# Selective scan in a four-layer kernel: softplus split between ScalarE, TensorE and VectorE, its steps placed anew, and one fill shared differently

## The chip, the cores and the metric

The kernel runs on one core of a Trainium2 chip. The metric is the device time of one launch in microseconds; lower is better. The engines are named as the profile names them: PE is TensorE, DVE is VectorE, ACT is ScalarE, POOL is GpSimd, SP is SyncE, which here only issues transfers (DMAs).

## The reference

The reference takes an image batch of 3 x 256 x 48 x 48 in fp32 through four layers, each added to its own input: an attention block with feed-forward parts, a 3 x 3 convolution with routed weights, a plain 3 x 3 convolution, and a state space (selective scan) layer. The change lies in the last one. Cut to what matters:

```python
xz = einsum('blc,dc->bld', layer_norm(group_norm(x)), in_proj_w)     # L = 2304 tokens, 256 channels
x_in, z = split(xz)                                                  # 512 inner channels each
u  = silu(causal_conv4(x_in))
dt_raw, B_ssm, C_ssm = split(u @ x_proj_w.T)                         # 16 + 16 + 16
dt = softplus(dt_raw @ dt_proj_w.T + dt_proj_b)                      # 512 channels
for t:                                                               # 16 states per channel
    h = h * exp(dt[t] * A) + dt[t] * B_ssm[t] * u[t]
    y[t] = (h * C_ssm[t]).sum(states)
out = ((y + u * D) * silu(z)) @ out_proj_w.T
```

The softplus of a value a is computed as max(a, 0) + ln(1 + exp(-|a|)).

## The kernel before, in words

Three layers come first and take the span up to about 2,020 us. The scan layer then works through 18 chunks (three images, six chunks of CH = 384 tokens each). The 512 inner channels are four blocks of 128 (m = 0 to 3). A block is taken in two steps (h = 0 and 1), so a chunk has eight steps; each step holds eight scans ("parts", g over two groups, q over four quarters of the block's channels), so that a partition of a scan holds one state of one channel.

In a step, ACT computes `decay` (exp of dt times A, L1811) into one of three PSUM slots, three parts ahead; DVE runs the recurrence as one scan instruction per part (L1819) in the tile `hs`; POOL multiplies the eight results by C (`times_c`, L1836); PE folds the products into `ps_y` (`add_states`, L1853). The input term dt*u*B of the next step is put into `hs` by `fill` at the end of a step: DVE fills the quarters 0 and 1 (`fill_upper`, L1765) from PSUM, POOL the quarters 2 and 3 (L1785). In the second step of a block POOL also does a part of DVE's share, the "second fill" (L1780), from a copy of the rows (`spread_second`, DMA `dtuq`). The rows of dt and dt*u reach the layout of the scan over DRAM: `keep_dt` stores them (`dtd`, `dtud`), `spread` loads them replicated (`dtr`, `dtur`), `spread_pe` does a part by PE.

Beside the scans of chunk `at`, the next chunk (rel = 1) and the one after it (rel = 2) are prepared. The list `plan` says where: an entry (j, place, rel, stage) puts a stage at half step j (0 to 15; j = 4m + 2h + part // 4), at a place BEGIN, MID, DONE, LATE (after the parts 0, 1, 2, 3 of that half step), or PE_ (after part 3 of a step, or, for odd j, at the end of the step). The stages that matter here are `group_scale` (L1213), `less_mean` (L1222), `centre` (L1235, L1237), `square_mean` (L1229), `inverse_root` (L1241, L1242) and `normalise` (L1246) for rel = 2, and `project_dt` (L1318), `softplus` (L1327 to L1329), `take_dt` (L1343, L1344) and `keep_dt` (L1349 and two DMAs) for rel = 1, the last four twice, for the blocks 0, 1 (m0 = 0) and 2, 3 (m0 = 2). All of them use the same two PSUM banks, `bank[0]` and `bank[1]` (in the profile `ps_g`): a stage that writes a bank follows the readers of the one before.

`keep_busy` (L1336) are filler matmuls with no result that is used; the table `busy` says after which parts they come. At the end `keep_order` ties the instructions of PE, DVE, ACT and POOL in this stage to the order in which the program lists them. SP's order is left to the planner of the framework. [...] Before the stage, the first chunk is prepared by another function with the same `softplus` and `take_dt`.

## Time and profile before

| | |
|---|---|
| median of 3 runs | 3367.3 us (3366.03 to 3369.35) |
| the profiled execution, its own time | 3369.11 us |
| its span | 3367.4 us |
| granted PE clock, mean | 0.978 |
| busy share of the span: PE, DVE, ACT, POOL | 94%, 86%, 71%, 40% |
| scan stage, 2018 to 3345 us: busy PE, DVE, ACT, POOL | 1199.7, 1311.0, 1098.4, 1283.5 us |
| one chunk in the stage (start to start of L1246) | 73.87 us |

The shares of the whole span mix the stages; POOL's 40%, for one, comes almost wholly from the last 1,330 us. Times of single instructions are durations, and consecutive instructions of an engine overlap somewhat, so that the distance from start to start is the cost of one. "Idle before" and an arrow name what an engine was waiting for.

### The profile page before, as it was taken

Reading aid. Unit: us, or ns where it says so; the run is one execution under the profiler, and the core shown is the slowest. Engines: PE = TensorE matmul, PEld = TensorE weight load, DVE = VectorE, ACT = ScalarE, POOL = GpSimd, SP = SyncE. Lnnn points to the kernel's source line nnn. Section 1 sums busy time; section 2 is a strip of 40 time slices with the busy share of each in tenths; the row PEclk is TensorE's granted clock in tenths of the full one; section 3 lists DMA queues with packets and bytes.
Section 4 is the critical chain, followed back from the end, with each engine's and each line's share of the span. In section 5 each row is a group of like instructions: output and inputs, shape, how many; then the busy total and the mean of one; then the engine's idle time right before and its main releaser. Section 6 shows DMA issues by size and latency. Waiting matters only on the chain.

```text
span 3367.4 us, 54979 instructions
## 1 busy us (share of the span) xinstructions
PE 3159.9 (94%) x21314; PEld 1591.0 (47%) x21314; DVE 2892.8 (86%) x3302; ACT 2376.1 (71%) x3596; POOL 1346.1 (40%) x457
## 2 busy tenths in 40 slices
PE   7999999999999999979999997999999999999995
PEld 4334343352333434547777763444444444444442
DVE  3799989958989998369975459999999999999997
ACT  2688888838888886331324447888888888888874
POOL 0000000000000000220000009999999999999997
PEclk9999999999999999989999999999999999999987
DMA  4000000010000002566611135455555555555552
GB/s 165 31 8 10 8 8 6 8 46 5 8 7 8 10 8 71 174 217 216 216 31 38 38 105 122 120 125 131 134 130 140 135 127 128 133 127 137 133 133 56
DMA packets 182164, 290.84 MB, mean 86 GB/s; under 512 B 34737, under 2 KB 148465, under 8 KB 179970
## 3 DMA queue, kind: packets, MB, share of 16 engines
q1 hardware_dynamic: 168658, 267.15, 29.4%
q10 hardware_dynamic: 13232, 20.06, 1.8%
q8 instruction: 169, 2.77, 0.4%
q14 instruction: 105, 0.86, 0.1%
HBM read 236.24 MB, written 50.64 MB: 85 GB/s over the span
## 4 chain that ended last, share of the span: by engine, by line
PE 52%; DVE 32%; ACT 7%; DMA 5%; issue 4%; SPq 1%; POOL 0%; ACTq 0%; DVEq 0%; POOLq 0%
DVE hs L1819 21%; PE ps_s L638 16%; PE acc L651 14%; PE ps_c L1546 8%; DVE hs L1765 3%; PE ps_s L1031 2%; DVE u L296 2%; PE ps_y L462 2%; ACT ps_da L1811 2%; PE ps_m L665 1%; PE ps_m L711 1%; PE acc L529 1%; PE ps_s L518 1%; DVE ps_g L1343 1%; PE ps_s L578 1%
## 5 line engine op out<-in xcount | busy, mean ns | idle before, releaser
L642 ACT ACTIVATE pt<-ps_s 128x1024 f32<-128x1024 f32 x972 | 942.5, 1022 | 154.6 <-PE ps_s L638 142.1
L1819 DVE TENSOR_TENSOR_SCAN hs<-ps_da,hs 128x385 f32<-128x385 f32 x1152 | 1002.1, 935 | 4.2 <-ACT ps_da L1811 1.5
L857 DVE TENSOR_TENSOR part<-part,pt 128x2048 f32<-128x2048 f32 x396 | 906.6, 2289 | 41.2 <-ACT pt L642 18.4
L1811 ACT ACTIVATE ps_da<-dtr,u 128x384 f32<-128x384 f32 x1152 | 656.6, 582 | 184.3 <-DVE hs L1819 175.7
L164 POOL TENSOR_TENSOR rstd<-ve,mhalf 128x2 f32<-128x2 f32 (+1 forms) x26 | 16.3, 629 | 1480.3 <-DVE ve L162 1480.3
L638 PE MATMUL ps_s<-q,kt 32*128 32x512 f32 (+1 forms) x4320 | 576.4, 592 | 0.1
L651 PE MATMUL acc<-pt,vt 128*32 128x512 f32 (+1 forms) x4320 | 520.9, 561 | 0.2
L1546 PE MATMUL ps_c<-vt,u 128*128 128x288 f32 x1728 | 432.4, 411 | 20.6 <-DVE u L263 20.6
L1836 POOL TENSOR_TENSOR hc<-hs,x 128x3072 f32<-128x3072 f32 x72 | 405.3, 5629 | 19.2 <-DVE hs L1819 15.2
L1836 POOL TENSOR_TENSOR hc<-hs,bc 128x3072 f32<-128x3072 f32 x71 | 399.9, 5633 | 15.9 <-DVE hs L1819 14.2
L1546 PEld LDWEIGHTS ps_c<-vt,u 128*128 128x128 f32 x1728 | 330.8, 192 | 117.1 <-issue 19.4
L638 PEld LDWEIGHTS ps_s<-q,kt 32*128 32x128 f32 x4320 | 195.2, 183 | 199.1 <-issue 120.2
L651 PEld LDWEIGHTS acc<-pt,vt 128*32 128x32 f32 x4320 | 94.4, 108 | 353.4 <-issue 326.7
L1853 PE MATMUL ps_y<-hc,u 128*32 128x384 f32 x2304 | 230.4, 521 | 2.8 <-POOL hc L1836 2.8
L1273 PE MATMUL ps_g<-u 128*128 128x384 f32 x576 | 195.2, 491 | 23.5 <-ACT u L1269 23.5
L1785 POOL TENSOR_TENSOR hs<-dtur,x 128x1536 f32<-128x1536 f32 x72 | 209.2, 2905 | 9.1 <-DMA dtur<-dtud 8.5
L1785 POOL TENSOR_TENSOR hs<-dtur,bc 128x1536 f32<-128x1536 f32 x72 | 209.3, 2907 | 1.1 <-DMA dtuq<-dtud 1.1
L1273 PEld LDWEIGHTS ps_g<-u 128*128 128x128 f32 x576 | 108.3, 191 | 107.2 <-ACT u L1269 34.7
L1336 PE MATMUL ps_r<-hs,ident 128*128 128x128 f32 x864 | 130.7, 292 | 19.8 <-DVE hs L1819 19.5
L1336 PEld LDWEIGHTS ps_r<-hs,ident 128*128 128x128 f32 x864 | 107.6, 192 | 73.8 <-DVE hs L1819 56.1
L1853 PEld LDWEIGHTS ps_y<-hc,u 128*32 128x32 f32 x2304 | 62.4, 113 | 145.0 <-issue 129.6
L1562 ACT COPY cb<-ps_c 128x288 f32<-128x288 f32 x48 | 19.2, 399 | 157.5 <-PE ps_c L1546 137.9
(266 smaller groups left out, 4062.8 us busy)
## 6 DMA issues: line engine op xcount, KB each, us to landing
wconv<-in_we SPq DMA_DIRECT2D x144, 384.0 KB, 4.4
dtr<-dtd SPq DMA_DIRECT2D x288, 192.0 KB, 3.9
dtur<-dtud SPq DMA_DIRECT2D x288, 96.0 KB, 4.2
wconv<-xd SPq DMA_DIRECT2D x36, 384.0 KB, 3.7
x<-bcd SPq DMA_DIRECT2D x72, 192.0 KB, 5.0
dtd<-x SPq DMA_DIRECT2D x36, 384.0 KB, 2.9
dtuq<-dtud SPq DMA_DIRECT2D x288, 48.0 KB, 2.0
bc<-bcd SPq DMA_DIRECT2D x72, 192.0 KB, 4.9
```

The lines of the kernel that those rows point to most:

```text
L638: nc.tensor.matmul(s[:, j, cols], kt[r, mt * P : (mt + 1) * P], q[r, :n], start=True, stop=True,)
L642: nc.scalar.activation(p[:, h0 : h0 + 2, :], s, AF.Exp)
L651: nc.tensor.matmul(acc[h * HD : (h + 1) * HD, :n], vt[:, mt, g * P + h * HD : g * P + (h + 1) * HD], p[:, h, cols], start=mt == 0, stop=mt ...
L857: ): nc.vector.tensor_tensor(part, first, p, ALU.add)
L1273: nc.tensor.matmul(bank[m % 2], w3v["taps"][:, m, tap, :], w3v["xi"][:, m % 3, tap : tap + CH], start=tap == 0, stop=tap == DCONV - 1,)
L1336: nc.tensor.matmul(spread_tiles[-1][:, i % 2, CH:], ident, src, start=True, stop=True)
L1546: nc.tensor.matmul(pc[:, :HN], u[:, i, dy, ct, m * P : (m + 1) * P], vt[:, i, ct, dy * TW : dy * TW + HN], start=ct == 0 and dy == 0, stop ...
L1785: nc.gpsimd.tensor_tensor(states(s)[:, :, 2:4, 1:], chunks[at].rows[m][1].unsqueeze(1).broadcast_to([P, 2, 2, CH]), b_rows(s, 0, 2), ALU.mult,
L1811: nc.scalar.activation(slots[n % 3][:, 1 : CH + 1], chunks[at].rows[m][0][:, q, :], AF.Exp, scale=amat[:, col : col + 1],)
L1819: nc.vector.tensor_tensor_scan(b, slots[(8 * s + part) % 3][:, : CH + 1], b, 0.0, ALU.mult, ALU.add)
L1836: nc.gpsimd.tensor_tensor(hc, tiles[s][:, :, :, 1:], cb.broadcast_to([P, 2, 4, CH]), ALU.mult)
L1853: nc.tensor.matmul(k.y_ps[32 * q : 32 * q + 32, :CH], fold, hc[:, g, q, :], start=False, stop=h == 1 and g == 1,)
```

## The change

In the scan stage `softplus` and `take_dt` are replaced by smaller stages. ACT writes the positive part max(a, 0) to the tile `dtu` (Relu) and |a| to `dt`; the exponential and the logarithm follow in place. PE adds the two by products with the identity matrix into the same banks (`sum_dt`, first the positive part, then the logarithm). DVE then only multiplies the bank by u (`take_sum`). The positions in the plan change with it: for m0 = 0 the bank is taken and stored at the end of the sixth step instead of in its first half; for m0 = 2 in the seventh step after part 4. `take_sum` stands ahead of `keep_dt`, as `take_dt` did. The first chunk, ahead of the stage, keeps `softplus` and `take_dt`, the latter without its fillers.

`group_scale` goes from the seventh step (one call for both halves) to the fourth, a half in each half step. `less_mean` moves from the end of the seventh step's first half to part 5 of that step. In the eighth step POOL's second fill covers one group instead of two, as in the other steps, and DVE's part of the fill ahead of it two quarters instead of one. Fillers go: those of `take_dt`, and eight of the 24 in the table. Both stores of B and C rows are issued ahead of the loads, and `keep_order` now covers SP as well.

```diff
-    def group_scale(k):
+    def group_scale(k, *cts):
         sc, sh = norm3[k.b]
-        for ct in range(CT):
+        for ct in cts or range(CT):
...
             nc.sync.dma_start(bcd[j], dbc[32 * (j + 1) : 32 * (j + 1) + DS, :])
+        for j in range(2):
             t = room(k, f"bc{j}")
...
+    def relu_of(k, m0):
+        for j in range(2):
+            nc.scalar.activation(k.dtu[:, m0 + j, :], bank[j], AF.Relu)
+
+    def abs_of(k, m0):
+        for j in range(2):
+            nc.scalar.activation(k.dt[:, m0 + j, :], bank[j], AF.Abs)
+
+    def relu_abs(k, m0):
+        for j in range(2):
+            nc.scalar.activation(k.dtu[:, m0 + j, :], bank[j], AF.Relu)
+            nc.scalar.activation(k.dt[:, m0 + j, :], bank[j], AF.Abs)
+
+    def exp_of(k, m0):
+        both = k.dt[:, m0 : m0 + 2, :]
+        nc.scalar.activation(both, both, AF.Exp, scale=-1.0)
+
+    def log_of(k, m0):
+        both = k.dt[:, m0 : m0 + 2, :]
+        nc.scalar.activation(both, both, AF.Ln, bias=1.0)
+
+    def sum_dt(k, m0, part):
+        src = (k.dtu, k.dt)[part]
+        for j in range(2):
+            nc.tensor.matmul(
+                bank[j], ident, src[:, m0 + j, :], start=part == 0, stop=part == 1
+            )
+
+    def take_sum(k, m0):
+        for j in range(2):
+            m = m0 + j
+            nc.vector.tensor_tensor(k.dtu[:, m, :], bank[j], k.u[:, m, :], ALU.mult)
...
             nc.vector.scalar_tensor_tensor(pdt, pdt, 0.0, k.dt[:, m, :], ALU.max, ALU.add)
             nc.vector.tensor_tensor(k.dtu[:, m, :], pdt, k.u[:, m, :], ALU.mult)
-            keep_busy(k.dtu[:, m, :P], 3)
...
-        (12, MID, 2, group_scale),
-        (12, PE_, 2, less_mean),
+        (6, BEGIN, 2, lambda k: group_scale(k, 0)),
+        (7, BEGIN, 2, lambda k: group_scale(k, 1)),
+        (13, MID, 2, less_mean),
         (13, DONE, 2, centre),
...
-        (9, LATE, 1, lambda k: softplus(k, 0)),
-        (10, DONE, 1, lambda k: take_dt(k, 0)),
-        (10, LATE, 1, lambda k: keep_dt(k, 0)),
-        (10, PE_, 1, lambda k: project_dt(k, 2)),
-        (11, LATE, 1, lambda k: softplus(k, 2)),
-        (12, MID, 1, lambda k: take_dt(k, 2)),
-        (12, DONE, 1, lambda k: keep_dt(k, 2)),
+        (9, DONE, 1, lambda k: relu_of(k, 0)),
+        (9, LATE, 1, lambda k: abs_of(k, 0)),
+        (10, BEGIN, 1, lambda k: sum_dt(k, 0, 0)),
+        (10, DONE, 1, lambda k: exp_of(k, 0)),
+        (11, BEGIN, 1, lambda k: log_of(k, 0)),
+        (11, MID, 1, lambda k: sum_dt(k, 0, 1)),
+        (11, LATE, 1, lambda k: take_sum(k, 0)),
+        (11, LATE, 1, lambda k: keep_dt(k, 0)),
+        (11, PE_, 1, lambda k: project_dt(k, 2)),
+        (11, PE_, 1, lambda k: relu_abs(k, 2)),
+        (11, PE_, 1, lambda k: exp_of(k, 2)),
+        (12, BEGIN, 1, lambda k: sum_dt(k, 2, 0)),
+        (12, BEGIN, 1, lambda k: log_of(k, 2)),
+        (12, MID, 1, lambda k: sum_dt(k, 2, 1)),
+        (13, BEGIN, 1, lambda k: take_sum(k, 2)),
+        (13, BEGIN, 1, lambda k: keep_dt(k, 2)),
...
-        busy = {(2, 0, 3): 4, (2, 1, 1): 3, (2, 1, 2): 3, (2, 1, 3): 3, (2, 1, 5): 3,
-                (3, 0, 0): 3, (3, 0, 1): 3, (3, 0, 2): 2}
+        busy = {(2, 0, 3): 4, (2, 1, 1): 2, (2, 1, 2): 2, (2, 1, 3): 3, (2, 1, 4): 3,
+                (3, 0, 3): 2}
...
                 fill_upper(s, 0, 2)
-                fill_upper(s + 1, 0, 1, 1 if m == DI - 1 else 2)
+                fill_upper(s + 1, 0, 1)
             else:
                 fill_upper(s, 1, 2, 1)
-                lo = 0 if m == DI - 1 else 1
                 nc.gpsimd.tensor_tensor(
-                    states(s)[:, lo:2, 1, 1:],
-                    chunks[at].second[m].unsqueeze(1).broadcast_to([P, 2 - lo, CH]),
-                    chunks[at].bc[0][:, 2 + lo : 4, :], ALU.mult,
+                    states(s)[:, 1, 1, 1:], chunks[at].second[m],
+                    chunks[at].bc[0][:, 3, :], ALU.mult,
                 )
...
-        keep_order(tc, listed, mark)
+        keep_order(tc, listed, mark, True)
...
-def keep_order(tc, listed, mark):
+def keep_order(tc, listed, mark, loads=False):
...
-    )
+    ) + ((mybir.EngineType.SP,) if loads else ())
```

## The prediction

> **What bounds the kernel now.** I read the page first: its slices show the last fifteen (2,020 us on) with DVE and POOL both at nine tenths. The changed functions run there. So the shares over the whole span decide nothing; that stretch does. Next the busy time by stretches (columns: stretch, length, busy time and count of PE, weight loads, DVE, ACT, POOL, then granted clock, DMA share, GB/s):

> ```profile
> 2600.00:2800.00 200.00, 186.81 (x922) 96.52 (x922) 198.46 (x239) 169.77 (x335) 193.52 (x54) 1.00 0.55 133
> 2800.00:3000.00 200.00, 185.09 (x938) 97.77 (x937) 198.36 (x244) 166.92 (x329) 193.74 (x56) 0.99 0.55 134
> ```

> The reader is to see that DVE is full (99%), and that the next two are close: POOL 97%, PE 93%. ACT has 84%. A microsecond taken from DVE counts until one of these stops it. Successive starts of the normalise line L1246 (2683.5, 2757.4, 2831.3 us) give the clock of the stage: one chunk every 73.87 us.

> Then the timeline of DVE over the third step pair of a chunk and what follows (start, length of the run, engine, line, count):

> ```profile
> 2804.81 2.65 DVE L1819 TENSOR_TENSOR_SCAN hs<-ps_da,hs 128x385 f32<-128x385 f32 x3
> 2807.64 0.57 DVE L1343 SCALAR_TENSOR_TENSOR ps_g<-ps_g,x 128x384 f32<-128x384 f32 x1 [0.18 <-ACT x L1329]
> 2808.24 0.56 DVE L1344 TENSOR_TENSOR dtu<-ps_g,u 128x384 f32<-128x384 f32 x1
> 2808.71 0.56 DVE L1343 SCALAR_TENSOR_TENSOR ps_g<-ps_g,x 128x384 f32<-128x384 f32 x1
> 2809.30 0.56 DVE L1344 TENSOR_TENSOR dtu<-ps_g,u 128x384 f32<-128x384 f32 x1
> 2809.78 4.35 DVE L1819 TENSOR_TENSOR_SCAN hs<-ps_da,hs 128x385 f32<-128x385 f32 x5
> 2814.04 0.53 DVE L1860 TENSOR_TENSOR x<-ps_y,x 128x384 f32<-128x384 f32 x1
> 2814.49 2.21 DVE L1765 TENSOR_TENSOR hs<-ps_r,x 128x1536 f32<-128x1536 f32 x2
> ```

> Instructions overlap, so what one costs is the distance of starts, not its duration: a scan 0.852 us (duration 0.935), the L1343/L1344 quartet 9.78 - 7.64 = 2.14 us, of which two L1344 take 0.47 each and two L1343 0.60. There is no idle time but 0.18 us.

> POOL at the end of the same chunk, and ACT and PE around the hand-over that the change makes later:

> ```profile
> 2819.88 1.55 POOL L1780 TENSOR_TENSOR hs<-dtuq,x 128x768 f32<-128x768 f32 x1
> 2821.39 2.91 POOL L1785 TENSOR_TENSOR hs<-dtur,x 128x1536 f32<-128x1536 f32 x1
> 2825.82 5.63 POOL L1836 TENSOR_TENSOR hc<-hs,x 128x3072 f32<-128x3072 f32 x1 [1.53 <-DVE hs L1819]
> ```
> ```profile
> 2822.48 2.85 PE L1222 MATMUL ps_g<-wconv,u 128*128 128x384 f32 x8 [0.31 <-ACT x L1349]
> ```
> ```profile
> 2825.36 0.85 ACT L1235 COPY wconv<-ps_g 128x384 f32<-128x384 f32 x2
> 2826.24 0.84 ACT L1237 ACTIVATE wconv<-wconv 128x768 f32<-128x768 f32 x1
> 2826.99 0.57 ACT L1811 ACTIVATE ps_da<-dtr,u 128x384 f32<-128x384 f32 x1
> ```

> POOL waits once a chunk, 1.53 us, for DVE: that is its whole slack. Eight matmul rows of a 384-wide product take 2.85 us, and the page counts two rows per product, so one product costs 0.71 us. The four products of less_mean (L1222) so end at 2825.33, and centre's copies (L1235) begin at 2825.36 behind a decay: nothing waits there now, but with no room to spare.

> [...] two Abs of L1327 take 0.85 us, 0.43 each; I price Relu at that. [...] POOL's L1836 stays at 5.63 us; so I price no contention. [...] The 3 us stretch from 2805 shows 0.57 while the rest of this chunk shows 1.00: [...] rival B rests on it.

> **The change part by part**, per chunk in microseconds; the dt work of a next chunk runs 17 times in the stage, the fills 18 times.

> 1. The positive part and the sum leave DVE. Four L1343 go: twice 2.14 becomes twice 0.97 (two products of bank and u, at L1344's 0.47 to 0.49): **-2.34**. The 0.18 wait for Ln goes if the sum is ready (below): **-0.18**.
> 2. Second fill. In the eighth step POOL's L1780 shrinks from 1.55 to the 0.87 of the other steps (-0.68 POOL); DVE's second L1765 before it grows from 384 to 768 per partition. In the same trace the pair takes 2.13 (2814.49 to 2816.62) where it has 384 and 2.53 where it has 768: **+0.40 DVE**, 18 times.
> 3. PE gets eight identity products, 8 x 0.71 = +5.7, and loses fillers: 12 of take_dt and 24 - 16 = 8 of the table, at 1.5 us for six, 20 x 0.25 = -5.0. Net +0.7 on about 69 busy. This lies beside DVE; it would be 69.5 of 72, still under DVE.
> 4. ACT gets four Relu, 4 x 0.43 = +1.7, on 62: 64 of 72. Group scaling (two L1213, 1.29) moves from the seventh step to the fourth; there decays run at most three scans ahead, and after the scan of part 4 ACT has a slack of about one scan (0.85) per 0.65 us inserted, so I cost it nothing; if that cover is gone, the Silu and its two table loads behind it (4.05) come up to 0.6 late, in front of a fill of 2.5.
> 5. Order on SP. It now follows the program. Both bcd stores stand ahead of all eight bc loads, and four dtuq loads behind them instead of two on each side: 0.83 of issue moves about 3.7 later. Those rows are next read by POOL over 10 us later. The dtd and dtud stores of blocks 0 and 1 move from the sixth step's middle to its end, directly ahead of the spread loads of the next chunk. Store 2.9 to 4.5, eight issues 3.7, load 3.9 to 4.3 (page): 12 to 15 us from the end of the sixth step. First reader is the decay for the next chunk, late in the eighth: by the pitches 2.5 + 0.97 + 2.53 + 6.82 + 0.97 + 5 = about 19. Hidden. What it replaces was a queue that stood: before, SP's 17 waits for L1349 lasted 109.8 us in the 600 us from 2600.
> 6. New waits. dt*u of blocks 0, 1 follows the sixth step's last scan. Ln follows the decay of part 4, ends about 1.5 after that scan, and two products give bank 1 at +3.0; DVE gets there after three scans and the gate, at +3.0. No wait, margin about 0.1. For blocks 2, 3 (seventh step, after scan 4) the sum is ready some 0.3 early. Then the bank is copied by ACT (L1349, 0.85) and only then less_mean may write it: four products, 2.85. From scan 4's end: decay 0.7, first copy 1.1, products to 4.0; centre's second copy is due at 3.7. ACT so stands 0.3 to 0.5 and the decay behind centre and square comes that much later. In the trace before, this decay ended 0.15 before its scan: the wait reaches DVE. I take **+0.45**; ends 0 (less_mean keeps ahead) and +1.2 (the standing repeats at inverse_root, whose square_mean is behind it).

> POOL's floor by starts: 8 x 5.59 + 8 x 2.86 + 4 x 0.83 = 70.9. DVE's: 64 x 0.852 + 4 x 2.53 + 4 x 0.45 (fills) + 4 x 0.45 (gates) + 0.85 (L1246) + 1.94 = 71.0 before any wait. They touch: DVE gains nothing below 71, and without the halved second fill POOL would have needed 71.6.

> Sum: 17 x (-2.34 - 0.18 + 0.45) + 18 x 0.40 = -35.2 + 7.2 = **-28.0 us**, a chunk of 72.2. The profiled execution took 3369.11 us (span 3367.4 and 1.7 around it); the median of the runs is 3367.3, 1.8 lower. So 3341.1 for a profiled run, **3339 us** for the median.

> **Rivals.**
> A, above (0.70): DVE stays the bound; with the ends of the new wait, -15 to -36, so 3331 to 3352.
> B (0.13), gain cut short: the fillers that are gone let PE's clock fall in another 3 us stretch of the sixth and seventh steps, where PE is busy only 9.7 of 12 us (2814 to 2826) and waits on ACT. At half speed that delays PE by up to 1.5 us; DVE has about 0.3 of margin at the sums, so some 1.2 more per chunk, 17 x 1.2 = 20: about 3359, at the edge of no change. Against: eight real products fill the same place. With POOL at its floor it ends similarly.
> C (0.13), slower: ACT's queue. From less_mean through centre, square, square_mean and inverse_root ACT waits for PE three times with the decays behind it. If less_mean starts 2 us late, say behind the second sum's products and add_states, centre stands that long, and each chunk gets 2.0 + 0.45 of stall where it won 2.1. It decides from a stall of 2.1 per chunk; at 3.0, 17 x 0.9 = +15: 3382. For it: PE is at 100% for 27 us before (2772 to 2799), so a delay is recovered slowly. Against: PE's idle time is precisely in these two steps.
> D (0.04): the order by program gives the same placement of DVE work but SP stands behind a store and the spread loads land late; the -28 is eaten: 3367.

> **How the numbers follow.** A measurement of this kernel tells about 0.2%, 6.7 us: faster is below 3360.6. A gives 0.70 there, B about 0.10, together 0.80; same is the rest of B and most of D, 0.06; slower C and a little of D, 0.14. The range 3327 to 3363 takes A's ends, 4 us for the pitches on the low side, and B; C is left out, 0.14, and about 0.04 below.

> **What would show it.** L1246's later line should start every 72.2 us (71.7 without new waits). DVE: no scalar_tensor_tensor in the stage, products of about 0.47 between starts, a wait ahead of the scans of the eighth step near 0.5. POOL's 1.53 wait in the seventh step should all but vanish. A stage longer than 73.9 per chunk with ACT idle for ps_g ahead of centre shows C; a clock below 0.9 in the sixth and seventh steps shows B; a DVE product that waits for PE's sum by over 0.5 refutes point 6.

## The result, and the profile after

The changed kernel takes 3336.7 us (median of four runs, 3329.3 to 3338.9) against 3366.7 for the kernel before on the same chip: a ratio, estimated from all runs, of 0.9906, 95% interval 0.9892 to 0.9919. The profiled execution has a span of 3333.4 us, 34.0 less than before.

The 34.0 us lie in three places. The scan stage, from the semaphore just ahead of DVE's first fill to DVE's first product with C in the last step, went from 1328.4 us (2016.6 to 3345.0) to 1300.5 (2012.1 to 3312.6): **-27.9 us**. It began 4.5 us earlier, and 1.6 us are saved behind it. In the fourteen kernels of the table below, whose earlier layers are the same, the stage began anywhere from 2007.8 to 2017.1 us, so those 4.5 us are scatter. The stage length of a profile is therefore the finer measure for what follows; it comes from one execution each.

By stretches, in the columns of the table shown before:

```profile
2600.00:2800.00 200.00, 188.40 (x906) 94.43 (x898) 198.69 (x238) 178.02 (x355) 197.70 (x58) 1.00 0.55 132
2800.00:3000.00 200.00, 189.58 (x884) 94.48 (x884) 197.59 (x235) 174.29 (x342) 196.38 (x57) 0.99 0.53 131
```

DVE is as full as before (99%); POOL went from 97% to 98.5%, ACT from 84% to 88%, PE from 93% to 94.5%. Successive starts of normalise are 72.25 us apart on average where they were 73.9. But the distances are of two kinds: ten of fifteen lie at 71.8 to 72.0, five at 72.8 or 72.9.

A chunk of the short kind, DVE's timeline from the end of the sixth step into the eighth:

```profile
2863.46 1.02 DVE L1355 TENSOR_TENSOR x<-ps_g,x 128x384 f32<-128x384 f32 x2
2864.39 2.62 DVE L1808 TENSOR_TENSOR hs<-ps_r,bc 128x1536 f32<-128x1536 f32 x2
2866.91 4.36 DVE L1860 TENSOR_TENSOR_SCAN hs<-ps_da,hs 128x385 f32<-128x385 f32 x5
2871.18 1.01 DVE L1355 TENSOR_TENSOR x<-ps_g,x 128x384 f32<-128x384 f32 x2
2872.09 2.66 DVE L1860 TENSOR_TENSOR_SCAN hs<-ps_da,hs 128x385 f32<-128x385 f32 x3
2874.66 0.55 DVE L1808 TENSOR_TENSOR hs<-ps_r,bc 128x384 f32<-128x384 f32 x1
2875.10 1.81 DVE L1860 TENSOR_TENSOR_SCAN hs<-ps_da,hs 128x385 f32<-128x385 f32 x2
2877.18 3.69 DVE L1860 TENSOR_TENSOR_SCAN hs<-ps_da,hs 128x385 f32<-128x385 f32 x4 [0.27 <-ACT ps_da L1852]
```

The two products with u (L1355, take_sum) start 0.93 us before what follows them, 0.47 each, with no wait; nothing is left of the scalar_tensor_tensor. The one wait, 0.27 us in the eighth step, is for a decay on ACT. On ACT, at the same moment, the copies of centre wait for PE's less_mean:

```profile
2874.67 0.48 ACT L1235 COPY wconv<-ps_g 128x384 f32<-128x384 f32 x1 [0.15 <-PE ps_g L1222]
2875.32 0.48 ACT L1235 COPY wconv<-ps_g 128x384 f32<-128x384 f32 x1 [0.17 <-PE ps_g L1222]
```

The long kind differs in one instruction: DVE waits for PE's sum in the seventh step.

```profile
2938.88 4.35 DVE L1860 TENSOR_TENSOR_SCAN hs<-ps_da,hs 128x385 f32<-128x385 f32 x5
2944.18 1.20 DVE L1355 TENSOR_TENSOR dtu<-ps_g,u 128x384 f32<-128x384 f32 x2 [0.94 <-PE ps_g L1348]
```

PE's timeline says why. The two chunks have the same instructions, but the fold of the states (L1894, 16 rows) takes 1.50 us in the short chunk and 2.51 in the long one. The eight rows of the sum behind it take 2.85 us in the short chunk and 2.19 + 1.45 in the long one. The first and the third line are the short chunk's:

```profile
2866.90 1.50 PE L1894 MATMUL ps_y<-hc,u 128*32 128x384 f32 x16
2938.87 2.51 PE L1894 MATMUL ps_y<-hc,u 128*32 128x384 f32 x16
2868.33 2.85 PE L1348 MATMUL ps_g<-x,ident 128*128 128x384 f32 x8
2941.30 2.19 PE L1348 MATMUL ps_g<-dtu,ident 128*128 128x384 f32 x4
2943.34 1.45 PE L1348 MATMUL ps_g<-x,ident 128*128 128x384 f32 x4
```

And the granted clock (the third column from the end) in the same two places:

```profile
2868.00:2871.00 3.00, 3.00 (x16) 1.63 (x9) 3.00 (x4) 2.80 (x6) 3.00 (x1) 1.00 0.45 138
2940.00:2943.00 3.00, 3.00 (x15) 1.09 (x8) 3.00 (x4) 2.80 (x6) 3.00 (x2) 0.56 0.75 159
```

In stretches of 1 us the clock falls under 0.8 at 2072, 2144, 2506, 2577, 2939 and 3011 us, and nowhere else between 2060 and 3230. DVE's 0.9 us waits for the sum number six in the stage, one at each of these.

### The profile page after: what moved, and what is told of

The parts are those of the page before. It is cut to its first block, busy times and chain, and to the rows that moved or that the text cites. A ratio compares the mean times of both kernels' runs of the same rounds, so it can differ in the third digit from the quotient of the medians.

```text
span 3333.4 us, 54144 instructions
## 1 busy us (share of the span) xinstructions
PE 3141.3 (94%) x20890; PEld 1555.3 (47%) x20890; DVE 2862.1 (86%) x3234; ACT 2393.7 (72%) x3664; POOL 1334.0 (40%) x457
## 4 chain that ended last, share of the span: by engine, by line
PE 56%; DVE 29%; ACT 8%; issue 4%; DMA 3%; POOL 0%; SPq 0%; ACTq 0%; DVEq 0%; POOLq 0%
DVE hs L1860 20%; PE ps_s L638 16%; PE acc L651 14%; PE ps_c L1589 8%; DVE hs L1808 3%; ACT ps_da L1852 2%; PE ps_s L1031 2%; PE ps_y L462 2%; DVE u L296 2%; PE ps_m L665 2%; PE ps_m L711 1%; PE acc L529 1%; PE ps_s L518 1%; PE ps_g L1222 1%; DMA wconv<-in_we 1%
## 5 line engine op out<-in xcount | busy, mean ns | idle before, releaser
L1860 DVE TENSOR_TENSOR_SCAN hs<-ps_da,hs 128x385 f32<-128x385 f32 x1152 | 1003.0, 940 | 5.8 <-ACT ps_da L1852 4.0
L1589 PEld LDWEIGHTS ps_c<-vt,u 128*128 128x128 f32 x1728 | 330.4, 192 | 118.2 <-issue 20.4
L1894 PE MATMUL ps_y<-hc,u 128*32 128x384 f32 x2304 | 227.3, 515 | 1.1 <-POOL hc L1877 1.1
L1273 PE MATMUL ps_g<-u 128*128 128x384 f32 x576 | 195.0, 491 | 23.3 <-ACT u L1269 23.3
L1894 PEld LDWEIGHTS ps_y<-hc,u 128*32 128x32 f32 x2304 | 62.1, 112 | 142.4 <-issue 129.6
L1392 PE MATMUL ps_g<-u 128*128 128x384 f32 x288 | 109.2, 513 | 13.0 <-ACT sz L1400 7.7
```

What stands on the lines that cost most here:

```text
L1273: nc.tensor.matmul(bank[m % 2], w3v["taps"][:, m, tap, :], w3v["xi"][:, m % 3, tap : tap + CH], start=tap == 0, stop=tap == DCONV - 1,)
L1392: nc.tensor.matmul(bank[j], w("in", ct * 512 + m * P, P), k.xn[:, ct, DCONV - 1 :], start=ct == 0, stop=ct == CT - 1,)
L1589: nc.tensor.matmul(pc[:, :HN], u[:, i, dy, ct, m * P : (m + 1) * P], vt[:, i, ct, dy * TW : dy * TW + HN], start=ct == 0 and dy == 0, stop ...
L1860: nc.vector.tensor_tensor_scan(b, slots[(8 * s + part) % 3][:, : CH + 1], b, 0.0, ALU.mult, ALU.add)
L1894: nc.tensor.matmul(k.y_ps[32 * q : 32 * q + 32, :CH], fold, hc[:, g, q, :], start=False, stop=h == 1 and g == 1,)
```

## The experiments

All stage lengths are counted as above, each from one profiled execution. Expectations that quote the changed kernel at 1300.2 us begin at the fill itself, 0.3 us later. Those that quote it at 1298.3 us, or two others at 1289.3 and 1289.6, end at a semaphore 2.2 us earlier: add 2.2 to compare. The ratio is against the kernel before, estimated from all runs.

| kernel | stage us | chunk us, mean | ratio, 95% interval |
|---|---|---|---|
| before | 1328.4 | 73.90 | |
| changed | 1300.5 | 72.25 | 0.9906 (0.9892 to 0.9919) |
| take_sum twice | 1350.0 | 75.10 | 1.0049 (1.0032 to 1.0065) |
| second fill as before | 1291.5 | 71.67 | 0.9866 (0.9849 to 0.9882) |
| scaling in step seven | 1307.2 | 72.71 | 0.9924 (0.9907 to 0.9940) |
| softplus as before | 1348.8 | 75.16 | 1.0040 (1.0029 to 1.0052) |
| SP by the planner | 1299.9 | 72.18 | 0.9912 (0.9895 to 0.9928) |
| fillers behind the fill | 1408.0 | 78.51 | 1.0226 (1.0209 to 1.0243) |
| filler table of before | 1319.9 | 73.31 | 0.9965 (0.9953 to 0.9978) |
| centre later | 1291.9 | 71.66 | 0.9874 (0.9857 to 0.9890) |
| second fill as before, centre later | 1291.8 | 71.71 | 0.9880 (0.9865 to 0.9895) |
| fillers ahead of the fill | 1301.2 | 72.25 | 0.9903 (0.9887 to 0.9918) |
| both, and fillers ahead | 1291.3 | 71.47 | 0.9871 (0.9855 to 0.9886) |
| split softplus alone | 1320.7 | 73.31 | 0.9969 (0.9957 to 0.9981) |

**take_sum twice.**

```diff
             nc.vector.tensor_tensor(k.dtu[:, m, :], bank[j], k.u[:, m, :], ALU.mult)
+            nc.vector.tensor_tensor(k.dtu[:, m, :], bank[j], k.u[:, m, :], ALU.mult)
```

> The changed kernel, with each of take_sum's four products per chunk computed twice (same values). Theory A (DVE sets the chunk, the other engines follow within a microsecond): each extra product costs its distance of starts, 0.47 us, 4 x 17 = 68 of them: the stage from first fill to last C product grows by 32 us (30 to 34), the run goes to about 3368. Rival (POOL's floor of 70.9 us a chunk or PE sets it and DVE has hidden slack): under 15 us.

The stage grew by 49.5 us: DVE sets the chunk, but neither number of theory A holds. In DVE's timeline:

```profile
2970.81 0.55 DVE L1355 TENSOR_TENSOR dtu<-ps_g,u 128x384 f32<-128x384 f32 x1
2971.39 0.56 DVE L1356 TENSOR_TENSOR dtu<-ps_g,u 128x384 f32<-128x384 f32 x1
...
2982.20 0.56 DVE L1355 TENSOR_TENSOR dtu<-ps_g,u 128x384 f32<-128x384 f32 x1 [2.42 <-PE ps_g L1348]
```

Two products that write the same rows one after the other start 0.58 us apart, not 0.47, so four of them take 2.10 us where two took 0.93: 2 x 17 x 1.17 = 40. The other 10 go with more waiting: DVE's waits for the sum, 5.5 us in the changed kernel (six waits), are 17.7 here (twelve).

**Second fill as before.**

```diff
-                fill_upper(s + 1, 0, 1)
+                fill_upper(s + 1, 0, 1, 1 if m == DI - 1 else 2)
...
+                lo = 0 if m == DI - 1 else 1
...
-                    states(s)[:, 1, 1, 1:], chunks[at].second[m],
-                    chunks[at].bc[0][:, 3, :], ALU.mult,
+                    states(s)[:, lo:2, 1, 1:],
+                    chunks[at].second[m].unsqueeze(1).broadcast_to([P, 2 - lo, CH]),
+                    chunks[at].bc[0][:, 2 + lo : 4, :], ALU.mult,
```

> The changed kernel with the eighth step's second fill as before (POOL 768 wide, DVE's second fill 384 wide). DVE loses 0.40 us a chunk, POOL gains 0.68, so POOL's floor by starts is 71.6 us. Theory A (the floors touch): POOL's floor takes over, a chunk of 71.6 to 72.3, the stage within -5 to +4 us of the changed kernel's 1300.2, and POOL without idle time. Rival (POOL is not near being the bound): the stage is shorter by 18 x 0.40 = 7 us and POOL still waits for DVE.

The stage is 9.0 us shorter than the changed kernel's: this part of the change costs time. That is the rival's direction; but POOL has no idle time left, as theory A had it (columns as above).

```profile
2600.00:2800.00 200.00, 190.65 (x903) 96.10 (x904) 198.14 (x239) 178.28 (x355) 200.00 (x57) 0.99 0.57 138
```

71.67 us a chunk is the predicted floor of POOL, 71.6. Theory A made a slip: it measured from the changed kernel, whose mean of 72.25 was 0.65 above that floor, so the floor left room for the gain. 0.40 of DVE's time times 18 is 7.2. The other 1.8 fit DVE's waits over the stage: those for the sum went from 5.5 us to 0.6, those for decays from 4.0 to 7.0.

**Scaling in step seven.**

```diff
-        (6, BEGIN, 2, lambda k: group_scale(k, 0)),
-        (7, BEGIN, 2, lambda k: group_scale(k, 1)),
+        (12, MID, 2, group_scale),
```

> The changed kernel with group_scale back in the seventh step (one call after part 1). Theory A (ACT's queue is full in that step): 1.29 us ahead of decays 5 to 7 push the copies of keep_dt, less_mean and centre about 1 us later, and DVE waits about 0.7 to 1.0 us per chunk for a decay behind centre: +11 to +16 us in the stage, ACT idle for PE ahead of centre. Rival (the ACT time is hidden there as it was before): within 2 us of the changed kernel.

+6.7 us, by the predicted chain, at half the price. ACT's and DVE's timelines of one chunk:

```profile
2734.34 0.48 ACT L1235 COPY wconv<-ps_g 128x384 f32<-128x384 f32 x1 [0.73 <-PE ps_g L1222]
```
```profile
2736.85 3.69 DVE L1859 TENSOR_TENSOR_SCAN hs<-ps_da,hs 128x385 f32<-128x385 f32 x4 [0.84 <-ACT ps_da L1851]
```

0.84 us of wait took the place of 0.27: DVE's waits for decays are 8.9 us over the stage, 4.0 in the changed kernel, and those for the sum 6.8 instead of 5.5.

**Softplus as before**, the rest of the change kept; `take_dt` has its fillers again.

```diff
-        (13, MID, 2, less_mean),
+        (12, PE_, 2, less_mean),
...
-        (9, DONE, 1, lambda k: relu_of(k, 0)),
...
-        (13, BEGIN, 1, lambda k: keep_dt(k, 2)),
+        (9, LATE, 1, lambda k: softplus(k, 0)),
+        (10, DONE, 1, lambda k: take_dt(k, 0)),
...
+        (12, DONE, 1, lambda k: keep_dt(k, 2)),
```

> The changed kernel with softplus and take_dt (its fillers included) in their old places and less_mean at its old place: all other parts of the change stay. Theory A (the gain is the four scalar_tensor_tensor): DVE has 2.34 + 0.18 more a chunk and not the new waits; the stage is that of the kernel before plus the wider DVE fill, 1328 + 18 x 0.40 = 1335 us, the run 3366 to 3376, no faster than before. Rival (the gain comes from the order of the loads, the earlier scaling or the lighter fillers): the stage stays under 1315.

1348.8 us, not 1335: the stage is longer than that of the kernel before by 20.4 (the medians of the runs differ by 15.1). So without the split the other parts lose. The fill accounts for 7.2. For the rest the waits of PE give a hint, in 600 us from 2600:

```profile
PE ps_r L1370 <- DVE dtu L1378: 14.0, 8, 3.4
PE ps_r L1370 <- DVE x L1378: 14.0, 8, 3.4
```

The fillers of take_dt wait up to 3.4 us for DVE's product, 28 us in all; in the kernel before the same two waits sum to 2.8. Between 2060 and 3230 us the clock falls 21 times, in the kernel before 5 times. Which of the two made the other was not tried.

**SP by the planner.**

```diff
-        keep_order(tc, listed, mark, True)
+        keep_order(tc, listed, mark)
```

> The changed kernel without SP in keep_order: the planner places the DMA issues. Theory A (transfers are hidden either way): the stage within 3 us of 1300.2. Rival (the order of the loads carries part of the gain): the stage longer by over 5 us, with waits of POOL or ACT for dtur, dtuq or dtr.

1299.9 us against 1300.5, no difference that one execution of each could tell: the loads are hidden in either order.

**Fillers behind the fill.** Five more fillers for PE's gaps in the sixth step.

```diff
+        (11, BEGIN, 1, lambda k: keep_busy(ident, 2)),
         (11, MID, 1, lambda k: sum_dt(k, 0, 1)),
...
+        (11, PE_, 1, lambda k: keep_busy(ident, 3)),
         (11, PE_, 1, lambda k: project_dt(k, 2)),
```

> The changed kernel with five fillers more per chunk, placed where PE stands idle in the sixth step: two ahead of the second product of sum_dt (idle 0.59 us), three ahead of project_dt of blocks 2 and 3 (idle 0.89 us). Theory B' (PE's clock falls to half for one window after these gaps in about six of the chunks, which then take 72.85 us instead of 71.97): the fall goes away or moves, the chunks are all about 72.0 and the stage is 4 to 5 us shorter, with no DVE wait of 0.9 us for sum_dt. Rival (the 0.9 us come from work at the image borders, not from the clock): the same six chunks stay long, stage within 1 us.

107.5 us longer. The place PE_ of an odd half step comes after the fill, and a filler writes into the PSUM tile that the fill reads:

```profile
PE ps_r L1370 <- DVE hs L1810: 29.0, 16, 3.4
```
```profile
ACT x L1334 <- PE ps_g L1319: 21.0, 8, 5.3
ACT dtu L1334 <- PE ps_g L1319: 19.0, 8, 5.2
```
```profile
DVE hs L1862 <- ACT ps_da L1854: 69.0, 37, 4.3
```

PE's filler waits for DVE's fill; project_dt comes behind it in PE's order; Relu waits for project_dt on ACT, up to 5.3 us; the decays stand behind Relu; DVE waits for them, 69 us over the stage (the first three lines count 600 us from 2600, the last the stage). It says nothing on the clock, but shows what a late start of project_dt costs: 6.3 us a chunk.

**Filler table of before.**

```diff
-        busy = {(2, 0, 3): 4, (2, 1, 1): 2, (2, 1, 2): 2, (2, 1, 3): 3, (2, 1, 4): 3,
-                (3, 0, 3): 2}
+        busy = {(2, 0, 3): 4, (2, 1, 1): 3, (2, 1, 2): 3, (2, 1, 3): 3, (2, 1, 5): 3,
+                (3, 0, 0): 3, (3, 0, 1): 3, (3, 0, 2): 2}
```

> The changed kernel with the filler table of before (24 instead of 16 per chunk, some at the start of the seventh step). Theory A: PE work rises by 8 x 0.25 = 2.0 us a chunk to about 71 of 72; the eight at parts 0 to 2 of the seventh step stand ahead of or between the products of sum_dt for blocks 2 and 3, which then come about 1 us late: DVE waits 0.5 to 1 us a chunk for them, stage +8 to +17 us. Rival (clock matters more than PE time): the falls of the clock go away and the stage is up to 5 us shorter.

+19.4 us. Chunks alternate, 72.5 and 74.2; in the long ones the clock falls and six fillers stand ahead of the sum:

```profile
2806.28 2.54 PE L1894 MATMUL ps_y<-hc,u 128*32 128x384 f32 x16
2808.76 1.52 PE L1370 MATMUL ps_r<-hs,ident 128*128 128x128 f32 x6
2810.11 1.45 PE L1348 MATMUL ps_g<-dtu,ident 128*128 128x384 f32 x4
2811.41 0.83 PE L1370 MATMUL ps_r<-hs,ident 128*128 128x128 f32 x6
2812.07 1.46 PE L1348 MATMUL ps_g<-x,ident 128*128 128x384 f32 x4
```
```profile
2812.92 1.20 DVE L1355 TENSOR_TENSOR dtu<-ps_g,u 128x384 f32<-128x384 f32 x2 [2.27 <-PE ps_g L1348]
```

So once softplus is split the lighter table carries a good part of the change's gain. On the kernel before it was not tried alone.

**Centre later.**

```diff
-        (13, DONE, 2, centre),
+        (13, LATE, 2, centre),
...
-        (14, MID, 2, inverse_root),
+        (14, DONE, 2, inverse_root),
```

> The changed kernel with centre one part later (after the last part of the seventh step) and inverse_root one part later. Theory A (a normal chunk loses 0.27 us because ACT stands for less_mean ahead of centre): that wait goes, the stage is 3 to 5 us shorter if nothing behind gets late; the next to come late is normalise's inverse root. Rival (the later square and root push the decays of the eighth step): DVE waits there for ACT by 0.3 to 1 us a chunk, stage up to 15 us longer.

-8.6 us. The 0.27 wait is gone: in 600 us from 2600 DVE waits for nothing but

```profile
DVE hs L1808 <- ACT wconv L1417: 1.9, 9, 0.2
DVE dtu L1355 <- PE ps_g L1348: 0.9, 4, 0.2
```

The gain is about twice the expected one, because the waits of 0.9 us for the sum are gone too. The clock still falls, every second chunk, but one step earlier (at 2780 us the fold behind the fifth step takes 2.7 us), where no sum is due.

**Second fill as before and centre later together**, the two edits shown above in one kernel.

> The wide second fill on POOL together with the later centre and inverse_root. Each alone gave a stage of 1289.3 and 1289.6 us against the changed kernel's 1298.3. Theory P (POOL's floor by starts, 71.6 us a chunk with the wide fill, binds): no further gain, every chunk 71.6 us or more, stage 1286 to 1290, POOL without waits. Rival (DVE binds, POOL only looks full): the gains add up, chunks of 71.0 to 71.2, stage 1280 to 1283.

1291.8: no more than either part alone. Theory P holds for the sum, not for "every chunk": chunks are 71.0 to 72.6 and only their mean is 71.7. POOL waits 1.5 us in the 1,150 us from 2100 to 3250, in the changed kernel 18. DVE's idle time, though, is again the wait for the sum: 7.8 us over the stage, 1.8 in centre later, and between 2060 and 3230 us the clock falls 11 times, there 8 times. How much each of the two holds the mean is not told apart here.

**Fillers ahead of the fill**, two at each place.

```diff
+        (11, BEGIN, 1, lambda k: keep_busy(ident, 2)),
         (11, MID, 1, lambda k: sum_dt(k, 0, 1)),
+        (11, LATE, 1, lambda k: keep_busy(ident, 2)),
         (11, LATE, 1, lambda k: take_sum(k, 0)),
```

> The changed kernel with four fillers more in PE's two idle gaps of the sixth step, now placed ahead of the step's fill so that none waits for it. Theory B' (half clock for one window after these gaps costs 0.85 us in six chunks): no chunk of 72.85, no 0.9 us wait of DVE for sum_dt, stage 4 to 5 us shorter, 1293 to 1295. Rival (fillers at this place delay project_dt or the fill whatever they wait for): stage longer by over 5 us, as in the trial with the fillers behind the fill.

1301.2: neither. The stage is no longer and no shorter, and the clock falls all the same, in five chunks (2361, 2494, 2795, 2928, 3156 us), which are the five long ones. So the fall costs 0.9 us per chunk as theory B' said, but PE's gaps of the sixth step alone do not explain it: in the 3.4 us ahead of these five falls PE was 87% or 88% busy. What they share with all others is worked out in the last section.

**Both, with the fillers**: second fill as before, centre later, and the four fillers ahead of the fill.

> Wide second fill, later centre and inverse_root, and the four fillers ahead of the fill. Theory P: POOL's floor of 71.6 holds, chunks of 71.6 throughout, stage 1285 to 1288, within 2 us of the kernel without the fillers. Rival (DVE binds): 1278 to 1282.

1291.3 us, 71.47 a chunk. It shows how POOL's floor acts. Most chunks take 71.0, below the floor, while POOL's own distance from second fill to second fill is 71.6: POOL falls 0.6 us behind each chunk. After seven chunks PE's fold waits for POOL's product. A fall of the clock begins at the same time, at 2626.7 us, and lasts three times as long as the others of this kernel between 2100 and 3220 us, 10.2 us. The sum is 4 us late, and one chunk takes 75.8; how much of it POOL and how much the clock made is not told apart:

```profile
2627.80 2.79 PE L1898 MATMUL ps_y<-hc,u 128*32 128x384 f32 x16 [1.05 <-POOL hc L1881]
```
```profile
2639.38 1.20 DVE L1355 TENSOR_TENSOR dtu<-ps_g,u 128x384 f32<-128x384 f32 x2 [3.96 <-PE ps_g L1348]
```

**Split softplus alone**, on the kernel before: the plan's new entries from `relu_of` to `keep_dt`, and

```diff
-        (12, PE_, 2, less_mean),
+        (13, MID, 2, less_mean),
```

> The kernel before with the split softplus and its places alone (relu, absolute value, sums by PE, take_sum, keep_dt, project_dt, less_mean as in the change); old filler table, group scaling in the seventh step, wide second fill on POOL, SP by the planner. If the effects of the parts simply add: the changed kernel's 1298.3 us of stage, -9 (wide fill), +6.6 (late scaling), +19.3 (old table), 0 (SP): 1315, 11 us under the kernel before. Rival 1 (the sum alone has the whole gain of 2.5 us a chunk on DVE): 1285 to 1295. Rival 2 (late scaling and late products of PE meet in the seventh step and multiply): over 1326, slower than before.

1320.7 us, 7.7 less than before. In the expectation's measure that is 1318.5 where adding the parts gave 1315. So the parts nearly add. Of the 27.9 us the split gives less than a third by itself, because DVE then waits for the sum (27 us from 2100 to 3250, in the changed kernel at most 5.5):

```profile
DVE dtu L1354 <- PE ps_g L1347: 18.7, 7, 2.7
DVE x L1354 <- PE ps_g L1347: 8.3, 8, 1.0
```

Its chunks have the two lengths, 72.5 and 74.2, of the kernel with the old filler table.

Four variants beat the changed kernel by about 9 us of stage, with medians of 3323.4 to 3327.9 us; the lowest is both with the fillers, ratio 0.9871. Between themselves they are not told apart, and the interval of the second fill as before with centre later still overlaps that of the changed kernel.

## Why the prediction was right, point by point

The forecast was 3339 us and a stage change of -28.0; measured were 3336.7 and -27.9 in the profiles, with a chunk of 72.25 for 72.2. That agreement is better than its terms, and in part luck (point 6).

- *Point 1*, four L1343 off DVE: right. The products cost 0.47, the wait for Ln is gone, DVE stayed the bound. In the trial that doubles them, a product that follows another on the same rows costs 0.58.
- *Point 2*, +0.40 for the wider fill: right in size, and the trial without it gives 9.0 for 7.2. The remark that POOL "would have needed 71.6" was right to 0.1 us, but the chunk never came down to that floor, so that halving the fill bought nothing here and cost those 9.0.
- *Point 3*, PE: +0.7 was too high (and makes 69.7, not 69.5). In 1,150 us of the stage, the kernel before first:

```profile
2100.00:3250.00 1150.00, 1073.73 (x5378) 559.92 (x5370) 1140.17 (x1384) 972.17 (x1897) 1116.81 (x316) 0.99 0.54 130
2100.00:3250.00 1150.00, 1082.94 (x5103) 541.45 (x5101) 1137.91 (x1355) 1005.56 (x1995) 1131.44 (x320) 0.99 0.56 135
```

PE is busy 1073.73 / 1150 x 73.9 = 69.0 us a chunk before and 1082.94 / 1150 x 72.25 = 68.0 after. Why it fell by 1.0 is not shown.
- *Point 4*, ACT: the four Relu add no table load (64 from 2100 to 3250 us in both kernels), and a pair of them (L1326, at 2855.54 us) takes 0.85 us, as the two Abs did from which it was priced. Scaling at no cost is right: DVE has no wait at its new place, and its old place would have cost 6.7.
- *Point 5*, the order of SP at nothing: right, 0.6 us. POOL's products with C take 5.63 to 5.64 us on average, as before, so no contention with DVE shows in them; the price of none was the author's estimate.
- *Point 6*, a wait of 0.45 behind centre: the mechanism is there, PE to ACT to DVE, at 0.27, in the chunks of the short kind. What was missed stands beside it: the sum of blocks 2 and 3 was to be "some 0.3 early", and with a clock of 0.50 (2940 to 2942 us) it is 0.9 late in six chunks, 5.5 us. By the prediction's own sign, a wait for the sum of over 0.5, the point is refuted in these six. Ten of the eleven short chunks have the 0.27. Over 17 chunks, 10 x 0.27 + 5.5 = 8.2, where 17 x 0.45 = 7.7 was booked: two terms were wrong and cancelled.
- *Rival B*: its effect came in a third of the chunks, a late sum behind a fall of the clock, at 0.9 instead of 1.2 us. Its reason, that the fillers which are gone let the clock fall, is not shown: with the table of before put back the clock falls 7 times between 2060 and 3230 us, in the changed kernel 6. The half speed it went by is what the kernel before shows from 2805 to 2807 us, 0.50. But PE stood idle for only 12% of the 3.4 us ahead of that fall, which starts at 2804.19. *Rival C* did not happen, but the chain it named is real: in the trial with fillers behind the fill it took 6.3 us a chunk.
- POOL's 1.53 us wait "should all but vanish": it shrank. In 1,150 us POOL's waits went from 33 to 18 us.

## What to carry to other kernels

When the fullest engine has been relieved by 2 us in 74, sum the next ones by distances of starts before giving work back to it: here POOL's sum said to 0.1 us where a chunk with the wide fill comes to stand, and two improvements of 9 us each did not add. Where the engines beside the full one are held to a listed order, as `keep_order` does here, the place of an instruction can count more than its duration: three fillers of 0.25 us, put behind a fill that reads the tile they write, cost 6 us a chunk, and moving two stages by one part each gained 9 us in all. And an engine that stays ahead on average can still lose time for carrying lag over chunks, so look at single periods and not at their mean alone.

## What the runs showed of the hardware that was not expected

How long PE was busy in the window does not decide. In the changed kernel PE was busy for only 57% of some windows, and no fall followed; in centre later each fall follows a window that was 88% busy. An estimate from the traces that goes by the form of the products sorts them. project_dt's have the form `17*128` in the lines below; the largest form in the stage is `128*128`. Take each matmul row at its length under the full clock (0.356 us for 384 wide, as eight take 2.85), times its form as a share of `128*128` (`17*128`: 0.13), add up a window and divide by 3.413. All 120 falls between 2060 and 3230 us follow windows of at most 0.41. Of the 4,511 other windows at full clock, three are that low. In the changed kernel the six windows ahead of a fall have 0.31 to 0.39, and no other has less than 0.41; in the kernel before the five have 0.34 to 0.40, and no other less than 0.44. That this sum makes the clock fall is not shown: no run was built to test it.

In the changed kernel a fall comes when the idle 0.89 us and project_dt of blocks 2 and 3 behind it lie, for the most part, in one window:

```profile
2864.58 1.55 PE L1319 MATMUL ps_g<-wconv,u 17*128 17x384 f32 x4 [0.89 <-ACT x L1382]
2936.54 1.55 PE L1319 MATMUL ps_g<-wconv,u 17*128 17x384 f32 x4 [0.89 <-ACT x L1382]
```

The windows around these two begin at 2864.12 and 2935.80 us, so that the second holds 0.74 us of the idle time, the first 0.46; the fall comes behind the second, at 2939.21. A chunk of 72.0 us is 21 windows and 0.3 us long, so the place in the window moves from chunk to chunk. In the six chunks with a fall project_dt starts 0.74 to 2.02 us into its window, in the other eleven at 0.02 to 0.48 or at 3.11 to 3.41. With SP by the planner it is the same: 0.67 to 1.90 us with a fall, at most 0.45 or at least 2.59 without. Four of the six falls (2506, 2577, 2939, 3011 us) come back there (2510, 2582, 2944, 3015); the first two do not, as their chunks lie otherwise in the windows. In three kernels with other chunks a fall comes every second chunk, 143 or 147 us apart, which is 42 or 43 windows. To keep project_dt's few rows away from a pause of PE would be the thing to try; no run did.

Two DVE products into the same rows start 0.58 us apart (take_sum twice, 2970.81 and 2971.39 us); two into different rows 0.47 (changed kernel, half of 2863.46 to 2864.39).
